# A masked sequence convolution in front of an fp8 feed-forward layer: x gathered in sorted order, transposed on TensorE, and convolved over the sequences that reach each chunk

## The chip, the cores and the metric

The kernel runs on one core of one Trainium2 chip. A time is the device time of one execution in microseconds (us); a kernel is given by the median of its runs. The engines are PE (TensorE: matmuls, with PEld for its weight loads), DVE (VectorE), ACT (ScalarE), POOL (GpSimd) and SP (SyncE, which here only issues DMAs). ACT and POOL issue DMAs too; all DMAs run on the same 16 DMA engines.

## The reference, cut to what matters

x has the shape [128 sequences b, 32 heads h, 512 positions l], float32, and each sequence b has a length between 78 and 453. Per head there is a response K of 512 values, made from a few small parameters; x is convolved with it causally, x times D is added, and positions at or beyond the sequence's length become zero. The result goes through a feed-forward layer along l (512 to 1376 to 512) whose inputs are rounded to fp8, and is added to x:

```
K = _get_kernel(log_dt, C, log_A_real, A_imag, Lq)            # [32 heads, 512]
y = irfft(rfft(u, 1024) * rfft(K, 1024))[..., :512] + u * D[:, None]
y = y * mask                                                  # l < length[b]
gate_out = fp8(y) @ gate_w.T ; up_out = fp8(y) @ up_w.T       # 512 -> 1376
hidden = silu(gate_out) * up_out
return x + fp8(hidden) @ down_w.T                             # 1376 -> 512
```

## The kernel before

The 32 heads are worked in 8 groups of 4 (`G`, `HG`); P is 128 and l is cut into 4 chunks of 128 (`LC`). The convolution is a block-Toeplitz product: output chunk c takes K's block of distance c-c' times input chunk c', for all c' up to c.

**Sorting.** The sequences are put in order of length, longest first: `rank` (L424 to L426), the permutation matrix `perm` (L427, bf16) and the row numbers `index` (L450, L452). Chunk c is then needed only for its first `CAPS[c]` sequences (128, 124, 84, 40; `NQ` = 376 columns in all instead of 512). A check at the end (`fits`, L442 to L444, and `verdict`) would send the whole computation to the second branch `wide` if the lengths did not fit; with these inputs it does not run.

**One group.** A group has three stages on PE:

1. Convolution of 4 heads (`conv`, L567, with `convolve`, L481). x comes transposed by the host (`xT`: [l, h, b]) in `load_x` (`xg`, one DMA of 1 MB per group), and the sum of chunks 0 and 1 comes as two accumulating DMAs on POOL's queue (`load_sums`, `xs`). x is the stationary operand, K's blocks `st` move (two DMAs per head, `toeplitz`, L470 and L471, that read a padded copy of K in DRAM, `kpads`). A product that two pairs of blocks share, `sp` (L485), is made once, copied by ACT (`shared`, L488), and added when DVE rounds the result to fp8 (`q`, L571). DVE then masks q by length (L581). The result is [b, l].
2. `sort` (L584): four fp8 matmuls per head with `perm` as the moving operand turn q into [l, sorted b] (`pq`), and ACT copies the 376 columns to `qs` (L596). `check_q` (L598) sums |q| on ACT to find numbers that are not finite.
3. `gate_up` (L625): 11 steps of 8 matmuls (L641, weights stationary, fp8 `qs` moving) into the PSUM tiles `gp` and `up`, two buffers each; ACT makes silu (`s`, L649), DVE the product (`v`, L651), and `quantise` (ACT L616, DVE L617 to L619) rounds it to `hq`. `Down.multiply` (L680) makes 11 matmuls of 512 columns per head from `hq`; `put_out` (L693) adds x (`xn`, gathered in the sorted order by `load_sorted`, an indirect DMA, L459) and scatters the rows to the output (L699, L697).

**Order.** The stages overlap by an order that is written out: the loop over g issues gate_up of group g, then, between the `down` matmuls of g, the convolution of g+1. `with after(x)` makes an instruction issue behind x on its engine. Work that isn't part of a group is strewn in: K of heads 4 to 15 (`others[0]`) in the prologue, K of heads 16 to 31 (`others[1]`) in groups 0 to 2, `low_halves` on ACT (L537).

**Queues.** SP issues the small inputs, `xg`, the weights and all of `st`. In group 0's gate_up, `first_loads` issues x of group 1 and both parts of `downT` from ACT (L116, L139, L144), and the sums and the first gather from POOL. In the prologue 22 matmuls that do nothing (`keep_busy`, L361) fill PE while K goes to DRAM and back.

**End.** The last group's output goes out in five scatters (three of 512 columns, two of 256, L697), each issued by POOL when its part is done.

Of the kernel before, what the change touches and what calls it, by code (L numbers as in the profile page):

```python
# [57 lines left out]
def ssm_fp8_ffn(  # L58
# [30 lines left out]
    CHUNKS = [3, 1, 2, 0]  # L89

# [8 lines left out]
    def chunk_of(g, c):  # L99
        return xT[c * P : (c + 1) * P, g * HG : (g + 1) * HG, :].rearrange("p h b -> p (h b)")  # L100


    def add_chunks(xg):
        xs = xp.tile([P, T], F32, name="xs", bufs=1)
        nc.vector.tensor_add(xs, xg[:, 0, :], xg[:, 1, :])
        return xs

    def load_sums(g):

        xs = xp.tile([P, T], F32, name="xs", bufs=1)  # L110
        nc.gpsimd.dma_start(xs, chunk_of(g, 1))  # L111
        return xs, nc.gpsimd.dma_start(xs, chunk_of(g, 0), accum_op=ALU.add)

    def load_x(g, queue=nc.sync):
        xg = xp.tile([P, LC, T], F32, name="xg", bufs=1)
        queue.dma_start(  # L116
            xg.rearrange("p c (h b) -> p c h b", b=B),
            xT[:, g * HG : (g + 1) * HG, :].rearrange("(c p) h b -> p c h b", p=P),
        )
        return xg  # L120

    sc = const.tile([P, 6], F32, name="sc")
    nc.sync.dma_start(sc, scales.to_broadcast([P, 6]))

    len_i = const.tile([P, B + 1], I32, name="len_i")
    nc.sync.dma_start(len_i[:, 0:B], lens.to_broadcast([P, B]))
    nc.sync.dma_start(len_i[:, B:], bass.AP(lens.tensor, lens.offset, [[1, P], [1, 1]]))
    x0 = load_x(0)
# [19 lines left out]
    load_gate_up(gw, gateT, 0, I2)  # L148

# [12 lines left out]

    RB, RZ = 2 * P // NB, P // NB
    NR = 2 * RB + NA
# [28 lines left out]
    gas = [kg.tile([P, w, NR + RZ], F32, name=f"ga{n}") for n, w in enumerate((HG, HB))]  # L193
# [44 lines left out]
    class Powers:  # L238
# [67 lines left out]
        def products(self):  # L306
# [6 lines left out]
            yield nc.vector.tensor_mul(sin, sin, self.be.unsqueeze(2).to_broadcast(S))  # L313

            ga = self.ga = gas[min(self.n, 1)][:, 0 : self.H, :]
            k0 = NR - NA
            yield nc.vector.tensor_add(ga[:, :, k0:NR], sin, cos)

            def pair(c0, step):
                a = ga[:, :, c0 : c0 + RB]  # L320
                return bass.AP(a.tensor, a.offset, [*a.ap[:-1], [step, 2], a.ap[-1]])


            yield nc.vector.tensor_sub(pair(0, RB), pair(k0, RB), pair(k0 + RZ, 0))

        def response(self, behind=None):
            kp = ps.tile([NR, self.H, NB], F32, name="kp", tag="dp")
            for j in range(self.H):
                nc.tensor.matmul(kp[:, j, :], self.ga[:, j, 0:NR], self.zb[:, j, :], start=j == 0, stop=False)
            done = nc.tensor.matmul(kp[:, :, NB - 1], last, sm[0:1, 5, self.hs], start=False, stop=True)  # L330
            kt = kts[self.n]
            with after(behind) if behind else ExitStack():
                copied = nc.vector.tensor_copy(kt[0:NR], kp)
            written = nc.sync.dma_start(kpads[self.n].rearrange("h (a b) -> a h b", b=NB), kt)
            return done, copied, written
# [25 lines left out]
    with after(done):  # L361
        keep_busy(22)
# [23 lines left out]
    l_i = kg.tile([P, L], I32, name="l_i")  # L386
    mask = const.tile([P, L], U8, name="mask")
# [3 lines left out]

    shared = [const.tile([P, 2, P], F32, name=f"shared{n}") for n in range(HG)]

    many = kg.tile([P, 1], F32, name="many")
    with after(first_done):
        nc.vector.memset(many, float(B))
    with after(coeffs_there):
# [4 lines left out]
        for t in shared:  # L402
            nc.gpsimd.memset(t[:, 1, :], 0.0)
        gpsimd_there = nc.gpsimd.tensor_scalar(key, lf, many, None, ALU.mult)
    with after(gpsimd_there):
        nc.gpsimd.tensor_add(key, key, col_f)
        for s, c in enumerate(CHUNKS):
            nc.gpsimd.iota(l_i[:, s * P : (s + 1) * P], pattern=[[-1, P]], base=(c + 1) * P - 1, channel_multiplier=0)
        mask_there = nc.gpsimd.tensor_scalar(mask, l_i, own, 255.0, ALU.is_lt, ALU.mult)
# [8 lines left out]
    perm = const.tile([P, B], BF16, name="perm")  # L418
    number = kg.tile([P, 1], BF16, name="number")
    counted = kg.tile([P, B], F32, name="counted")  # L420
    index = const.tile([P, 1], I32, name="index")
    with after(copied):
        xs0 = add_chunks(x0)
# [4 lines left out]
    with after(mask_there):  # L428
# [6 lines left out]
        nc.gpsimd.tensor_scalar(number, col_f[:, B:], -1.0, B - 1.0, ALU.mult, ALU.add)  # L435
        nc.gpsimd.iota(row_i, pattern=[[P, LC]], base=P - 1, channel_multiplier=-1)
        nc.gpsimd.tensor_copy(row_f, row_i)
# [8 lines left out]
    def indices(behind):  # L446

        op = ps.tile([P, 1], F32, name="op", tag="dp")
        with after(behind):
            nc.tensor.matmul(op, perm, number, start=True, stop=True)  # L450
        yield
        nc.vector.tensor_copy(index, op)  # L452

# [3 lines left out]
    def load_sorted(g):  # L457
        xn = xp.tile([P, HG * L], F32, name="xn", bufs=2)
# [6 lines left out]
    def toeplitz(pool, h):  # L465

        n = next(n for n, (_, h1) in enumerate(batches) if h < h1)
        st = pool.tile([P, 5, P], F32, name="st")
        kpad, at = kpads[n], kpads[n].offset + (h - batches[n][0]) * KP
        done = nc.sync.dma_start(st[:, 1:4, :], bass.AP(kpad.tensor, at + 5 * P, [[1, P], [1, 3 * P]]))  # L470
        done = nc.sync.dma_start(st[:, 0:5:4, :], bass.AP(kpad.tensor, at, [[1, P], [2 * P, 2], [1, P]]))  # L471
        return st, done

# [493 lines left out]
```

## Time and profile before

| | us |
|---|---|
| median of 3 runs (lowest to highest) | 312.45 (312.18 to 313.72) |
| the profiled execution | 312.24 |
| its span, first to last instruction | 310.5 |
| PE busy in the span | 286.3 |
| DVE busy | 264.7 |
| ACT busy | 183.7 |
| POOL busy | 47.2 |
| bytes moved by DMA | 48.48 MB |

In a row of the timeline the columns are the start, the duration, the engine, the line of the kernel, the operation, what it writes and reads, how many instructions were merged into the row, and in square brackets how long the engine had been idle and what released it. A matmul's recorded duration contains the way through the array, which overlaps with the next matmul; what a matmul costs in a stream is the distance from its start to the next one's start. A float32 matmul appears as two records (two passes), each with a weight load of its own.

### The profile page before, as it was taken

What the parts mean: (1) busy time and instruction counts of PE and PEld (TensorE: products, weight loads), DVE (VectorE), ACT (ScalarE), POOL (GpSimd) and SP (SyncE); (2) the same over time, 40 slices, a digit from 0 to 9 for tenths busy, and PEclk for the clock granted to TensorE, in tenths of its full rate; (3) what the DMA queues carried; (4) which work ended last, traced back from release to release, by engine and by line L of the source; (5) the groups of instructions that cost most, each with busy time, mean ns of one, the idle gap of its engine ahead of it and who ended that gap; (6) DMA issues with size and microseconds to landing.
All of it is one profiled execution on the core that took longest, in us unless ns stands there. A gap on an engine that the chain in (4) does not pass through costs nothing. (4 is left out here: it accounts for less than half of the span.)

```text
span 310.5 us, 4833 instructions
## 1 busy us (share of the span) xinstructions
PE 286.3 (92%) x1692; PEld 173.3 (56%) x1708; DVE 264.7 (85%) x465; ACT 183.7 (59%) x388; POOL 47.2 (15%) x96
## 2 busy tenths in 40 slices
PE   8999939995999999999999999999999999999870
PEld 3486517742577456745576457745674557555330
DVE  5895939795999999986999699969998799989980
ACT  5835725497855878288846486458816683578100
POOL 5740111021000210021003100030002110000042
PEclk9999987997999999999999999999999999999995
DMA  2599999594016930488036911593049640000033
GB/s 87 194 276 380 375 288 359 149 271 203 0 42 160 284 161 0 100 260 292 4 80 191 314 61 43 153 309 140 1 116 267 260 136 2 0 0 2 1 157 122
DMA packets 27987, 48.48 MB, mean 156 GB/s; under 512 B 3348, under 2 KB 17428, under 8 KB 26036
## 3 DMA queue, kind: packets, MB, share of 16 engines
q1 hardware_dynamic: 21940, 23.78, 26.9%
q0 software_dynamic: 4064, 20.45, 19.1%
q10 hardware_dynamic: 1952, 3.87, 3.4%
q8 instruction: 15, 0.25, 0.3%
q14 instruction: 16, 0.13, 0.1%
HBM read 39.55 MB, written 8.54 MB: 155 GB/s over the span
## 5 line engine op out<-in xcount | busy, mean ns | idle before, releaser
L680 PE MATMUL dp<-dw,hq 128*128 128x512 bf16 (+1 forms) x348 | 81.1, 380 | 3.9 <-DVE hq L619 2.4
L641 PE MATMUL gp<-qs,gw 128*128 128x512 fp8e4 (+1 forms) x352 | 71.7, 326 | 9.0 <-ACT s L649 8.4
L649 ACT ACTIVATE s<-gp,psc 128x512 f32<-128x512 f32 x88 | 58.7, 680 | 34.0 <-PE gp L641 27.8
L651 DVE SCALAR_TENSOR_TENSOR v<-up,psc,s 128x512 f32<-128x512 f32 x88 | 64.4, 748 | 16.0 <-ACT s L649 16.0
L641 PE MATMUL up<-qs,uw 128*128 128x512 fp8e4 (+1 forms) x352 | 71.9, 327 | 0.4
L680 PEld LDWEIGHTS <-hq 128*128 128x128 bf16 x363 | 33.1, 96 | 44.3 <-DVE hq L619 7.4
L618 DVE SCALAR_TENSOR_TENSOR hq<-m,v 128x1024 bf16<-128x1024 bf16 (+1 forms) x56 | 55.6, 993 | 1.1
L617 DVE SCALAR_TENSOR_TENSOR v<-m,v 128x1024 f32<-128x1024 bf16 (+1 forms) x56 | 55.4, 990 | 1.0 <-ACT m L616 1.0
L616 ACT ACTIVATE m<-v 128x1024 bf16<-128x1024 f32 (+1 forms) x56 | 48.7, 870 | 7.2 <-DVE v L651 7.1
L641 PEld LDWEIGHTS <-gw 128*128 128x128 bf16 x352 | 32.3, 98 | 35.8 <-issue 10.4
L641 PEld LDWEIGHTS <-uw 128*128 128x128 bf16 x352 | 32.5, 99 | 27.2 <-issue 2.6
L596 ACT ACTIVATE qs<-pq 128x376 fp8e4<-128x376 f32 x32 | 14.6, 479 | 28.0 <-PE pq L588 28.0
L693 DVE SCALAR_TENSOR_TENSOR xn<-dp,nsc,xn 128x512 f32<-128x512 f32 (+1 forms) x33 | 23.0, 730 | 8.8 <-PE dp L680 8.7
L488 ACT ACTIVATE shared<-sp,inv 128x128 f32<-128x128 f32 x32 | 11.5, 361 | 29.5 <-PE sp L485 29.5
L571 DVE SCALAR_TENSOR_TENSOR q<-cp,inv,shared 128x512 fp8e4<-128x512 f32 x32 | 23.8, 744 | 3.1 <-PE cp L494 2.9
L111 POOL DMA_DIRECT2D xs<-xT x7 | 4.4, 623 | 119.3 <-PE sp L485 119.2
L619 DVE TENSOR_SCALAR hq<-hq 128x1024 bf16<-128x1024 bf16 (+1 forms) x56 | 20.9, 373 | 1.4
L490 PE MATMUL cp<-st,xg 128*128 128x256 f32 x64 | 19.6, 388 | 0.0
L491 PE MATMUL cp<-st,xg 128*128 128x256 f32 x64 | 19.5, 387 | 0.0
L492 PE MATMUL cp<-st,xg 128*128 128x256 f32 x64 | 19.2, 382 | 0.0
L699 POOL DMA_INDIRECT out<-xn,index x7 | 7.6, 1084 | 75.3 <-DVE xn L693 70.9
L602 ACT ACTIVATE s<-q 128x1024 bf16<-128x1024 fp8e4 x16 | 16.7, 1054 | 0.0
(156 smaller groups left out, 286.5 us busy)
## 6 DMA issues: line engine op xcount, KB each, us to landing
xg<-xT SPq DMA_DIRECT2D x7, 1024.0 KB, 7.5
st<-kpad SPq DMA_DIRECT2D x32, 192.0 KB, 3.6
st<-kpad SPq DMA_DIRECT2D x32, 128.0 KB, 3.8
xs<-xT POOLq DMA_DIRECT2D x14, 256.0 KB, 5.1
dw<-downT ACTq DMA_DIRECT2D x2, 1280.0 KB, 8.0
gw<-gateT SPq DMA_DIRECT2D x2, 768.0 KB, 8.3
gw<-gateT SPq DMA_DIRECT2D x1, 1216.0 KB, 12.9
uw<-upT SPq DMA_DIRECT2D x1, 1216.0 KB
```

The source lines that it names most:

```text
L490: nc.tensor.matmul(cp[:, 1:4:2, :], xg[:, 0, b], st[:, 2:4, :], start=True, stop=False)
L491: nc.tensor.matmul(cp[:, 0:4:2, :], xg[:, 2, b], st[:, 2:4, :], start=False, stop=False)
L571: nc.vector.scalar_tensor_tensor(q[:, j, :].rearrange("p (k c l) -> p k c l", k=2, c=2), cp.rearrange("p (k c) l -> p k c l", k=2), inv[:, ...
L616: nc.scalar.activation(m, v, AF.Abs, scale=2.0**20 * (1.0 + 2.0**-6), accum_out=acc)
L617: yield nc.vector.scalar_tensor_tensor(v, m, 1.5 * 2.0**14, v, ALU.max, ALU.add)
L618: yield nc.vector.scalar_tensor_tensor(out, m, 1.5 * 2.0**14, v, ALU.max, ALU.subtract)
L619: yield nc.vector.tensor_scalar(out, out, FP8_MAX, -FP8_MAX, ALU.min, ALU.max)
L641: multiplied = nc.tensor.matmul(o[:, :, 0 : CAPS[c]], w[:, c, i * P : (i + 1) * P], qs[:, :, OFF[c] : OFF[c] + CAPS[c]], start=(c == 0), s ...
L649: gated = nc.scalar.activation(s, gp, AF.Silu, scale=pgate)
L651: done = nc.vector.scalar_tensor_tensor(v[:, (i - i0) * T : (i - i0 + 1) * T], up, pup, s, ALU.mult, ALU.mult)
L680: done = nc.tensor.matmul(self.dps[n], self.hq[:, i, j * B : (j + 1) * B], dm[:, i, l0:l1], start=(i == 0), stop=(i == IC - 1),)
L693: added = nc.vector.scalar_tensor_tensor(o, self.dps[n], ndown, o, ALU.mult, ALU.add)
```

## The change

- **x.** `xT` is read no more (outside `wide`). For each group the rows of x come once, in sorted order, by the indirect DMA that fetched them before for the final addition (`load_sorted`); for group 0 they come unsorted by a plain DMA first, and a second time sorted. Per head, four float32 transposes on TensorE (`by_length`: 128, 124, 84 and 40 rows of x stationary, an identity matrix moving) turn the needed sequences into [l, sorted b]; in group 0 four float32 matmuls with `perm` do it. ACT copies the 376 columns to SBUF (`take`).
- **Convolution.** K's blocks are now stationary and x moves: one float32 matmul of 376 columns for the diagonal, then six of 124, 84, 40, 84, 40 and 40 columns. The sum of chunks, the shared product, the subtraction in `products` and POOL's accumulating DMAs go away. The padded K is shorter, and `st` comes in one DMA of 256 KB per head, four in a row for a whole group (`load_k`).
- **Rounding.** ACT makes fp8 directly from PSUM into `qs` (`quantise_y`), and DVE masks 376 bytes per partition instead of 512. `sort` goes away; the mask is made in sorted order on DVE from a sorted copy of the lengths. `check_q` sums 752 columns instead of 1024 and runs for the group before.
- **Order.** Two heads' transposes stand at the start of the convolution stage, then 10 `down` matmuls, then the four convolutions with the other two heads' transposes between them.
- **Queues.** All weights, K and `downT` are loaded on SP's queue, in the order x of group 0, first parts of gate and up, K of group 0, the rest of gate and up, K of group 1, `downT`. ACT issues only the small inputs (at the very start). POOL issues the gathers, the write of the second K to DRAM and the scatters. The `xn` tile has three buffers, `qs` three.
- **Prologue and end.** `keep_busy(22)` becomes `keep_busy(7)`; the mask's work on POOL becomes work on DVE. The last group's output goes out in two scatters (1536 and 512 columns).

The core of the diff:

```diff
-    def load_sums(g):
-        xs = xp.tile([P, T], F32, name="xs", bufs=1)
-        nc.gpsimd.dma_start(xs, chunk_of(g, 1))
-        return xs, nc.gpsimd.dma_start(xs, chunk_of(g, 0), accum_op=ALU.add)
...
+    x0 = rows_of_x()
+    nc.sync.dma_start(x0, xb[0])
...
     load_gate_up(gw, gateT, 0, I2)
+    load_gate_up(uw, upT, 0, I1)
...
     with after(done):
-        keep_busy(22)
+        keep_busy(7)
...
+    sorted_lengths = ps.tile([P, B], F32, name="sl", tag="cp")
+    nc.tensor.matmul(sorted_lengths, lengths, perm, start=True, stop=True)
+    order = ps.tile([P, 1], F32, name="op", tag="dp")
+    nc.tensor.matmul(order, perm, number, start=True, stop=True)
...
+        st = pool.tile([P, LC, P], F32, name="st")
+        kpad = kpads[n]
+        return st, nc.sync.dma_start(st, bass.AP(kpad.tensor, kpad.offset + (h - batches[n][0]) * KP, [[1, P], [1, LC * P]]))
...
+            def by_length(g, j, xn):
+                xp_ = ps.tile([P, NQ], F32, name="xp", tag=("gp", "up")[j % 2])
                 for c in range(LC):
+                    o, n = xp_[:, OFF[c] : OFF[c] + CAPS[c]], CAPS[c]
+                    x = xn[:, j * L + c * P : j * L + (c + 1) * P]
+                    if g:
+                        done = nc.tensor.transpose(o, x[0:n], eye[0:n, 0:n])
+                    else:
+                        done = nc.tensor.matmul(o, x, perm[:, 0:n], start=True, stop=True)
+                return xp_, done
+
+            def take(xp_, before):
+                xt = xtp.tile([P, NQ], F32, name="xt")
+                with after(before) if before else ExitStack():
+                    return xt, nc.scalar.activation(xt, xp_, AF.Copy)
...
+            def conv(st, xt):
+                cp = ps.tile([P, NQ], F32, name="cp")
+                nc.tensor.matmul(cp, st[:, LC - 1, :], xt, start=True, stop=False)
+                for d in range(1, LC):
+                    for c in range(d, LC):
+                        done = nc.tensor.matmul(
+                            cp[:, OFF[c] : OFF[c] + CAPS[c]],
+                            st[:, LC - 1 - d, :],
+                            xt[:, OFF[c - d] : OFF[c - d] + CAPS[c]],
+                            start=False,
+                            stop=c == LC - 1 and d == LC - 1,
+                        )
+                return cp, done
+
+            def quantise_y(qs, j, cp, before, done):
+                with after(before) if before else ExitStack():
+                    made = nc.scalar.activation(qs[:, j, :], cp, AF.Copy, scale=inv[:, 0:1], saturate=False)
+                words = qs.bitcast(I32)[:, j, :]
+                with after(done) if done else ExitStack():
+                    return made, nc.vector.tensor_tensor(words, words, mask.bitcast(I32), ALU.bitwise_and)
...
             with after(loaded):
-                load_gate_up(uw, upT, 0, I1)
                 load_gate_up(gw, gateT, I2, IH)
                 load_gate_up(uw, upT, I1, IH)
                 load_gate_up(gw, gateT, IH, I)
-                load_gate_up(uw, upT, IH, I)
+                loaded = load_gate_up(uw, upT, IH, I)
+            with after(convolved):
+                others[0].response(done, nc.gpsimd)
+            with after(loaded):
+                sts, loaded = load_k(1)
+            with after(loaded):
+                load_down(0, EARLY)
+                load_down(EARLY, IC)
...
-            first_loads = {
-                2: lambda hq: loads.append(load_x(1, nc.scalar)),
-                3: sums_1,
-                5: lambda hq: loads.append(load_down(0, EARLY, nc.scalar)),
-                7: lambda hq: loads.append(load_down(EARLY, IC, nc.scalar)),
-                9: sorted_0,
-            }
+            first_loads = {3: rows(1, 0), 7: rows(0, firsts[1])}
...
+                for j in range(2):
+                    xp_, last = turn_head(j)
+                    xt, sent = take(xp_, sent)
+                    xts.append(xt)
+                for n in range(2):
+                    with after(last):
+                        last = d.multiply(n, 0, EARLY)
                 for j in range(HG):
+                    with after(last):
+                        cp, last = conv(sts[j], xts[j])
+                    if j < 2:
+                        xp_, last = turn_head(j + 2)
+                        xt, sent = take(xp_, sent)
+                        xts.append(xt)
                     if j in (0, 2):
                         with after(done):
                             *_, done = jobs.pop(0)
...
+                    sent, done = quantise_y(qs, j, cp, sent, done)
                 if g + 2 < G:
+                    sts, _ = load_k(g + 2)
+                    xns[g + 2] = load_sorted(g + 2)
...
+            check_q(G - 1, qs)
...
-    widths = [*(v.shape[1] for v in groups[:-1]), L, L, L, L // 2, L // 2]
+    widths = [*(v.shape[1] for v in groups[:-1]), 3 * L, L]
```

`rows(g, i)` issues the gather of group g's x from POOL once `hq[:, i]` of group 0 is there (a copy of one element on POOL waits for it); `turn_head(j)` calls `by_length` behind the last PE instruction.

## The prediction

> **What bounds the kernel now.** I read the page's busy times and slices first, to see which engine is full and where it is not:
>
> ```profile
> PE 286.3 (92%) x1692; PEld 173.3 (56%) x1708; DVE 264.7 (85%) x465; ACT 183.7 (59%) x388; POOL 47.2 (15%) x96
> ...
> PE   8999939995999999999999999999999999999870
> ...
> PEclk9999987997999999999999999999999999999995
> ```
>
> PE is full from slice 10 on. Its holes, and the slices with a low granted clock (PEclk), lie in the first quarter and at the end. So: the body is a sum of PE distances, the holes are waits. In the body gate_up starts at 174.34 us (group 4) and 271.61 (group 7), so a group takes 32.42 us; busy time by stretch gives PE 96.28 of these 97.27 us, an idle 0.3 us per group. Next the timeline, for what one head's convolution and sort cost PE there:
>
> ```profile
> 157.34 0.30 PEld L485 LDWEIGHTS sp<-st,xs 128*128 128x128 f32 x2
> ...
> 157.67 0.60 PE L490 MATMUL cp<-st,xg 128*128 128x256 f32 x2
> ...
> 158.10 0.59 PE L491 MATMUL cp<-st,xg 128*128 128x256 f32 x2
> ...
> 159.08 0.30 PEld L494 LDWEIGHTS cp<-st,xg 128*128 128x128 f32 x2
> ...
> 159.30 2.01 PEld L680 LDWEIGHTS <-hq 128*128 128x128 bf16 x10
> ...
> 163.52 0.32 PEld L588 LDWEIGHTS <-q 128*128 128x128 fp8e4 x4
> ...
> 163.77 0.30 PEld L485 LDWEIGHTS sp<-st,xs 128*128 128x128 f32 x2
> ```
>
> One convolution is 159.30 - 157.34 = 1.96 us, one sort 163.77 - 163.52 = 0.25: 2.21 us per head. A 256-column float32 matmul costs 158.10 - 157.67 = 0.43, or 0.84 ns per column and pass; a 128-column one 0.22 (159.08 to 159.30), 0.107 per pass. Then the first hole, on the same view, and the clock behind it in busy time by stretch:
>
> ```profile
> 39.56 0.80 PE L641 MATMUL up<-qs,uw 128*128 128x512 fp8e4 x4
> ...
> 43.76 0.38 ACTq L139 DMA_DIRECT2D dw<-downT  x1
> ...
> 44.81 1.27 ACT L649 ACTIVATE s<-gp,psc 128x512 f32<-128x512 f32 x2 [5.88 <-issue]
> ...
> 45.55 1.41 PE L641 MATMUL gp<-qs,gw 128*128 128x512 fp8e4 x4 [5.19 <-ACT s L649]
> ```
> ```profile
> 44.00:48.00 4.00, 2.45 (x8) 1.10 (x8) 2.47 (x4) 3.19 (x6) 0.00 (x0) 0.50 1.08 339
> 48.00:52.00 4.00, 4.00 (x19) 3.50 (x18) 3.35 (x6) 2.56 (x9) 1.09 (x1) 0.68 1.06 345
> ```
>
> ACT stood still until its DMA of downT was issued at 43.76 (DMA share about 1 there), so `s` was late, PE idled 5.19 us, and the granted clock (third number from the right) fell to 0.50. From 27.33 to 68.02, gate_up to gate_up, group 0 takes 40.69 us, 8.27 over the body's 32.42. Last, the end:
>
> ```profile
> 301.07 0.48 DVE L693 SCALAR_TENSOR_TENSOR xn<-dp,nsc,xn 128x256 f32<-128x256 f32 x1
> ...
> 304.54 0.97 POOL L697 DMA_INDIRECT out<-xn,index  x1 [0.30 <-issue]
> ```
>
> The last result is there at 301.55; POOL, at 1.28 us per scatter, issues the last one at 304.54.
>
> **The change, part by part.** Sums are made against the profiled run, 312.24 us (span 310.5 and 1.74 around it), 0.21 below the median of 312.45.
>
> *Convolution on PE.* 376 columns: 376 x 0.84 ns x 2 passes = 0.63 us. Six small ones (124 to 40 columns): no row has a float32 matmul with a full 128-column weight load and fewer than 128 moving columns. By columns alone they cost (124+84+40+84+40+40) x 1.68 ns = 0.69 us; if the weight load is the floor, each pass costs what a 128-column pass costs, 6 x 0.215 = 1.29. I take the floor: the float32 weight load is recorded at 190 to 195 ns for 128 columns and 112 ns for 32 columns (K's matmul, L329), so about 0.84 ns per column, 107 ns for 128. `keep_busy` has 52 weight loads for 51 matmuls with one weight, so a repeated weight is loaded again. Per head 1.92 (ends 1.32 and 1.92).
>
> *Transposes instead of sort.* Four per head, float32, not in the trace. Nearest rows: the fp8 sort, 0.062 each, and the two-pass float32 matmul, 0.215. I take one pass with a float32 weight load, 0.107, so 0.43 per head. Rows of the trace name the part of the array that is used (128*128, 128*32, 1*32); a 40-row transpose may use less than 128 rows. Where that part changes from 128*128 to 128*32 and to 1*32 (25.13 to 25.27, 26.02 to 26.15), PE lost 0.07 to 0.10. Two changes per head: 0.17. Together 0.60 (ends 0.25 and 0.86 + 0.17 = 1.03).
>
> The Trainium skill's page "TensorE: Matmul & The Clock Gate", section "Part 4: PE-mode transpose", speaks against this step: about 275 ns per bf16 transpose in a kernel, and the clock gate doesn't count it as work. By 275 ns the four would take 1.1 per head and not 0.43, and the sum below would be 19 us longer. No run so far shows a transpose; the 40-column fp8 matmul is recorded at 183 ns and costs 62, so I read 275 as a duration, not a distance.
>
> So a head takes 1.92 + 0.60 = 2.52 instead of 2.21, and a stage 4 x 0.31 = 1.24 more. DVE loses L571 (744 ns) and the mask shrinks from 292 ns (128 words) to an estimated 250 (94 words; 64 and 128 elements take DVE 225 and 279 ns): 0.79 per head, 3.1 per group, on an engine that is behind PE; the 0.3 us per group that PE idles should go (wait list: `hq` before L680). The two ACT copies per head (about 0.48 each by L596, for 0.36 + 0.48) lie beside PE: `xt` of heads 0 and 1 has 2.1 us of `down` matmuls as cover, that of 2 and 3 a convolution of 1.92; uncovered, each would cost 0.48. Net +0.94 per stage, 7 stages: **+6.6**.
>
> *Group 0.* ACT issues no DMA there, and xg, xs and a second x layout no longer move. From 17 us on the DMAs run at about 378 GB/s. K 1.05 MB and the rest of the weights 4.33 MB are in by about 31; the last of them is needed at 34. The 5.19 us wait and the slow clock go. What is late next: K of group 1, the gather of group 1 (issued at about 32 behind `hq[:,0]`, median 7.9 us to landing, so about 40) and half of downT, 3.4 MB, 9 us, against the first transpose at about 40. I reserve 0.8 (ends 0 and 5). The other wait of these groups, 3.25 us at 73.98, stays: ACT's sines wait for angles on DVE, which follow the put_outs. Gain 8.27 - 0.8: **-7.5**.
>
> The page "Trainium Kernel Development and Optimization", section "Key Constraints", says that queues share the 16 DMA engines and that several issuers save only issue time. Then the move to SP gives no bandwidth, and only the bytes count; the row above shows that the issue itself held ACT.
>
> *Prologue.* PE ends K's matmuls at 11.6; 7 fillers 1.5, order and 16 perm matmuls of 0.215 to about 17.0 (x0 and perm are there by 13.4), four convolutions 7.7, copy, mask and K's next batch about 1.4: gate_up at about 26.3 instead of 27.33, **-1.0**. 0.5 MB more ahead of K's round trip in SP's queue can take it back (ends 0 and -1.8). The four ACT copies are ahead of the sines; these wait for DVE anyway.
>
> *POOL and SP.* POOL loses 14 sum DMAs and the l mask; the gathers are issued a group ahead. SP's K loads come four in a row behind the weights; nothing else waits on SP. check_q of the last group lands on ACT, idle from 289: nothing; uncovered 2 us.
>
> *End.* Two scatters instead of five. The last would be issued at about 301.7, not 304.54, but the 2.1 MB of both groups move at up to 451 GB/s from 299.9 on and need until about 305, against 307.1 now: **-2.3** (ends 0 and -2.9).
>
> Sum: 312.24 + 6.6 - 7.5 - 1.0 - 2.3 = 308.0.
>
> **The rivals.**
> - *Transposes at the two-pass price* (ends slower). Place: the head of each convolution stage. 0.215 each plus the tile changes is 1.03 per head: +0.43 x 28 = +12.0, 320.0 us. It decides early: 4.2 us over 112 transposes, so above 0.145 each nothing is left, above 0.16 it is slower by 0.5%. For it: no single-pass float32 row exists. Against: only that a transpose does no arithmetic; no row.
> - *The clock drops in the stages.* By columns alone a head has 1.32 us of convolution and some 0.16 of transposes in 2.52 us, about 60% of PE's time. For it: after 3.25 us of idling the clock stood at 0.50 for some 3.4 us (74.7 to 78). Against: 56% busy (292.4 to 295.8) left it at 1.00. If each stage lost 1.7 us: +12, 320.
> - *The group-0 stall moves instead of going.* gather and downT arrive 5 us later than the first transpose: 308.0 + 4.2 = 312.2, no change. For it: POOL's 256 KB sum took 5 us at 33.4 under full DMA load.
> - *No weight-load floor.* 1.32 + 0.25 per head: 4 x (1.57 - 2.21) - 0.3 = -2.9 per stage, -20: 281. Against: the load durations above.
>
> **How the numbers follow.** 0.5% (1.56 us) is about what a measurement of this kernel tells from no change. Main case 0.50, of which nine tenths are under 310.9; transposes 0.16; clock 0.10; stall 0.12, half of it within 0.5%; no floor 0.07; 0.05 for a mishap that I don't see, slower. Faster 0.45 + 0.07 + 0.04 = 0.56, same 0.05 + 0.06 = 0.11, slower 0.33. Range: the good ends together (transposes 0.062 and no tile change, -9.8; reserve 0, prologue -1.8, end -2.9) give 312.24 - 3.2 - 8.3 - 1.8 - 2.9 = 296; I take 299, since not all fall together, and above the two slower rivals, 322. The main case alone: 304 to 311.
>
> **What would show it.** Right: no ACT wait for a DMA issue near 40 us and clock 1.00 there; gate_up of group 1 at about 60 instead of 68; a body of about 33.4 us per group; a small float32 matmul 0.215 from the next, a transpose 0.107; the last scatter issued near 302. Wrong: transposes 0.2 apart or more, PEclk below 9 in the stages, PE idle before the first transpose, `cp` or `xt` waits of PE on ACT.

## The result, and the profile after

The changed kernel takes 327.42 us (median of 4 runs, 326.61 to 328.22); the kernel before, in the same comparison, 312.89 (312.18 to 313.72). The ratio is 1.046, with a 95% interval of 1.042 to 1.050: slower, where 308.0 was forecast. The profiled execution has a span of 324.5 us, 14.0 more than before. Medians below are over all runs of a kernel, ratios leave out single runs more than 1.5% above the fastest of the same kernel (one each in e1, e4 and e6).

The page of the changed kernel, busy times and slices:

```profile
PE 296.8 (91%) x1776; PEld 176.0 (54%) x1776; DVE 240.4 (74%) x433; ACT 187.4 (58%) x388; POOL 31.2 (10%) x72
...
PE   6899934998899999999999999999999999999970
...
PEclk9999985999999999999999999999999999999996
```

DVE lost 24 us of work and PE gained 10.5. Between the first slice and the end PE has one large hole, in slices 6 and 7, and the granted clock falls only there. So the loss has two places: that hole, and something in the body that doesn't look like a hole.

The starts of gate_up, read from the timeline, cut both spans at the same points:

| | before | after | difference | forecast |
|---|---|---|---|---|
| up to the first gate_up | 27.33 | 28.05 | +0.7 | -1.0 |
| group 0 | 40.69 | 45.89 | +5.2 | -6.6 (-7.5 and one stage) |
| group 1 | 38.11 | 37.80 | -0.3 | +0.9 |
| groups 2 to 6 | 165.48 | 175.30 | +9.8 | +4.7 |
| last gate_up to the end | 38.89 | 37.45 | -1.4 | -2.3 |
| span | 310.5 | 324.5 | +14.0 | -4.2 |

Groups 3 to 5 are alike: 33.27 us before, 35.33 after. (The 32.42 per group of the prediction was a mean over groups 4 to 6, and group 6 lasts only 30.73, because its last `down` product moves behind the next gate_up. The body before was 0.85 longer than the prediction thought, and group 0's excess was 7.4 and not 8.27.)

Group 0 first. The timeline of SP's and PE's queues after:

```profile
34.34 3.72 SPq L437 DMA_DIRECT2D st<-kpad  x4
38.11 1.24 SPq L119 DMA_DIRECT2D dw<-downT  x2
39.39 4.48 SPq L124 DMA_DIRECT2D dw<-downT  x1
```
```profile
42.42 1.26 PE L502 MATMUL xp<-eye,xn 128*128 128x128 f32 x8
52.96 3.57 PE L631 MATMUL dp<-dw,hq 128*128 128x512 bf16 x8 [9.27 <-DMA dw<-downT]
```

The issue of downT from ACT is gone, and ACT waits for no issue there any more. In its place PE waits 9.27 us for downT itself, which SP issued only at 38.11, behind K's four blocks. The clock answers as it did before; by stretch (busy time of PE, PEld, DVE, ACT and POOL, granted clock, DMA share, GB/s):

```profile
44.00:48.00 4.00, 0.00 (x0) 0.00 (x0) 3.40 (x5) 1.46 (x5) 0.00 (x0) 0.77 1.02 404
48.00:52.00 4.00, 0.00 (x0) 0.00 (x0) 0.00 (x0) 0.00 (x0) 0.00 (x0) 0.50 1.01 406
52.00:56.00 4.00, 3.04 (x8) 1.06 (x8) 0.00 (x0) 0.00 (x0) 0.00 (x0) 0.50 0.87 289
```

Then the body; PE's timeline through one convolution stage (group 4), from the transposes of two heads to the next gate_up:

```profile
197.91 1.26 PE L502 MATMUL xp<-eye,xn 128*128 128x128 f32 x8
199.11 0.85 PE L631 MATMUL dp<-dw,hq 128*128 128x512 bf16 x3
200.16 1.75 PE L631 MATMUL dp<-dw,hq 128*128 128x512 bf16 x7 [0.21 <-DVE hq L567]
201.75 0.79 PE L526 MATMUL cp<-xt,st 128*128 128x376 f32 x2
202.38 1.43 PE L529 MATMUL cp<-xt,st 128*128 128x124 f32 x12
203.64 0.67 PE L502 MATMUL xp<-eye,xn 128*128 128x128 f32 x4
204.24 0.90 PE L526 MATMUL cp<-xt,st 128*128 128x376 f32 x2
204.98 1.43 PE L529 MATMUL cp<-xt,st 128*128 128x124 f32 x12
...
208.83 0.88 PE L526 MATMUL cp<-xt,st 128*128 128x376 f32 x2
209.55 1.43 PE L529 MATMUL cp<-xt,st 128*128 128x124 f32 x12
210.80 4.25 PE L631 MATMUL dp<-dw,hq 128*128 128x512 bf16 x18
215.24 3.79 PE L631 MATMUL dp<-dw,hq 128*128 128x512 bf16 x16 [0.20 <-DVE hq L567]
218.87 0.80 PE L589 MATMUL gp<-qs,gw 128*128 128x512 fp8e4 x4
```

By distances, four transposes cost 204.24 - 203.64 = 0.60. The 376-column product costs 202.38 - 201.75 = 0.63 where it follows `down`, 204.98 - 204.24 = 0.74 where it follows transposes, and 209.55 - 208.83 = 0.72 where it follows another convolution. The twelve small passes cost 203.64 - 202.38 = 1.26, 0.105 each, whether they have 124 columns, 84 or 40. Transposes and convolutions together are 10.25 us of this stage, 1.41 more than the 8.84 before (4 x 2.21). The 44 `down` matmuls have 10.71 against 10.06: the lists of waits, first of the changed kernel and then of the kernel before, have

```profile
PEld L631 <- DVE hq L567: 12.9, 21, 2.0
...
PE dp L631 <- DVE hq L567: 4.5, 14, 1.5
```
```profile
PEld L680 <- DVE hq L619: 7.4, 9, 2.0
```

(total, how often, the longest). 1.41 + 0.65 = 2.06, the whole difference of the body.

### The profile page after: what moved, and what is told of

Read it like the earlier page. It is cut to its first block, busy times and chain, and to the rows that moved or that the text cites. A ratio compares the mean times of both kernels' runs of the same rounds, so it can differ in the third digit from the quotient of the medians.

```text
span 324.5 us, 4852 instructions
## 1 busy us (share of the span) xinstructions
PE 296.8 (91%) x1776; PEld 176.0 (54%) x1776; DVE 240.4 (74%) x433; ACT 187.4 (58%) x388; POOL 31.2 (10%) x72
## 4 chain that ended last, share of the span: by engine, by line
PE 48%; DVE 29%; issue 8%; ACT 7%; DMA 6%; POOLq 0%; POOL 0%; SPq 0%; ACTq 0%; DVEq 0%
PE cp L529 12%; PE dp L631 12%; DVE v L599 9%; PE cp L526 7%; DVE v L565 6%; PE gp L589 6%; DVE hq L566 5%; PE up L589 5%; DMA dw<-downT 5%; ACT s L597 4%; DVE hq L567 3%; PE xp L502 3%; ACT m L564 2%; ACT qs L541 1%; DMA sm<-ssm 1%
## 5 line engine op out<-in xcount | busy, mean ns | idle before, releaser
L631 PE MATMUL dp<-dw,hq 128*128 128x512 bf16 (+1 forms) x363 | 86.2, 386 | 13.8 <-DMA dw<-downT 9.3
L631 PEld LDWEIGHTS <-hq 128*128 128x128 bf16 x363 | 33.8, 99 | 60.0 <-DVE hq L567 12.9
L529 PEld LDWEIGHTS cp<-xt,st 128*128 128x128 f32 x384 | 47.9, 192 | 8.1
L529 PE MATMUL cp<-xt,st 128*128 128x40 f32 (+2 forms) x384 | 45.7, 272 | 0.0
L544 DVE TENSOR_TENSOR qs<-qs,mask 128x94 int32<-128x94 int32 x32 | 8.2, 255 | 50.4 <-ACT qs L541 50.4
L510 ACT ACTIVATE xt<-xp 128x376 f32<-128x376 f32 x32 | 14.7, 481 | 47.7 <-PE xp L502 46.3
L649 POOL DMA_INDIRECT out<-xn,index x9 | 9.3, 1033 | 237.8 <-DVE xn L644 237.0
L541 ACT ACTIVATE qs<-cp,inv 128x376 fp8e4<-128x376 f32 x32 | 18.3, 571 | 22.1 <-PE cp L529 22.0
L526 PE MATMUL cp<-xt,st 128*128 128x376 f32 x64 | 27.8, 516 | 0.0
L502 PE MATMUL xp<-eye,xn 128*128 128x128 f32 (+1 forms) x112 | 18.3, 266 | 0.0
L502 PEld LDWEIGHTS xp<-eye,xn 128*128 128x128 f32 (+1 forms) x112 | 13.8, 150 | 4.3
```

Source lines behind the costliest of these rows:

```text
L502: done = nc.tensor.transpose(o, x[0:n], eye[0:n, 0:n])
L526: nc.tensor.matmul(cp, st[:, LC - 1, :], xt, start=True, stop=False)
L529: done = nc.tensor.matmul(cp[:, OFF[c] : OFF[c] + CAPS[c]], st[:, LC - 1 - d, :], xt[:, OFF[c - d] : OFF[c - d] + CAPS[c]], start=False, s ...
L631: done = nc.tensor.matmul(self.dps[n], self.hq[:, i, j * B : (j + 1) * B], dm[:, i, l0:l1], start=(i == 0), stop=(i == IC - 1),)
```

## The experiments

### downT ahead of K of group 1 (e1), and one gather later (e2)

The first theory for group 0: downT is late because it stands in SP's queue behind K's blocks, which wait for K's write. The rival: the bytes are too many, whatever their order.

```diff
             with after(loaded):
+                load_down(0, EARLY)
+                loaded = load_down(EARLY, IC)
+            with after(loaded):
                 sts, loaded = load_k(1)
-            with after(loaded):
-                load_down(0, EARLY)
-                load_down(EARLY, IC)
```

> Edit: in the changed kernel, SP issues the loads of downT right behind the gate and up weights, and K of group 1 after them. Nothing else. The changed kernel is at 327.4 us; there SP stood waiting for K's write to DRAM until 34.3 us, the DMAs were 0.20 busy from 32 to 36, downT was issued at 38.1 and was awaited by PE until 53.0 (9.3 us idle, then the clock at 0.50 until about 56). Theory H (downT is late because SP's queue was blocked in front of it): downT lands near 40, the 9.3 us wait and some 2 us of slow clock go, gate_up of group 1 starts near 63 instead of 73.9: 316 to 317 us. Rival R (the 16 DMAs have too much to move before 44 us: K 1, gathers 3, downT 2.8 MB): the wait only moves to K of group 1 or to the gather: 322 to 327 us.

319.95 us against 313.1 of the kernel before on that chip, ratio 1.018 (1.013 to 1.023); 7.5 less than the changed kernel. Group 0 fell from 45.89 to 38.22. The wait for downT is gone, as theory H said; its 316 to 317 us were not reached: the first gate_up came 1.1 later (29.13), and a shorter wait was left. What is late next is what the prediction had thought of, the gather of group 1. PE's timeline:

```profile
45.30 1.74 PE L502 MATMUL xp<-eye,xn 128*128 128x128 f32 x8 [1.63 <-DMA xn<-x,index]
```

The second run adds that the third gather (of group 2's x, which nothing needs for 30 us) waits on POOL for `hq[:, 7]`:

```diff
-                    xns[g + 2] = load_sorted(g + 2)
+                    with after(nc.gpsimd.tensor_copy(turn[:, 2:3], hq[:, firsts[4], 0:1])) if g == 0 else ExitStack():
+                        xns[g + 2] = load_sorted(g + 2)
```

> Edit: as the run before (downT ahead of K of group 1), and the gather of group 2's x, which POOL issued at 41 us right behind that of group 0, now waits for hq[:,7] of group 0. Theory H: the same 316 to 317 us, since what mattered was when downT was issued. Rival R (bytes): the third megabyte out of the way gives another 2.5 us where the run before still has a wait for a DMA in group 0, and nothing where it has none.

319.45 us, ratio 1.020 (1.016 to 1.024); group 0 37.72. The two runs can't be told apart. The order in the queue was the fault, not that gather.

### The 40-row transposes made 128 rows (e3)

PE's records name the part of the array that an instruction uses: 128*128, 124*128 and 84*128 for the first three transposes of a head, 40*128 for the last. The prediction had charged two changes of shape per head. Here the 40-row transposes get 128 rows; the extra columns aren't read:

```diff
-                xp_ = ps.tile([P, NQ], F32, name="xp", tag=("gp", "up")[j % 2])
+                xp_ = ps.tile([P, L], F32, name="xp", tag=("gp", "up")[j % 2])
...
-                        done = nc.tensor.transpose(o, x[0:n], eye[0:n, 0:n])
+                        if n < 64:
+                            n = P
+                        done = nc.tensor.transpose(xp_[:, OFF[c] : OFF[c] + n], x[0:n], eye[0:n, 0:n])
```

> Edit: the transpose of the fourth chunk takes all 128 rows of x (into spare columns of the PSUM bank) and not 40, so that all four have the same tile 128*128. In the changed kernel the distances in one head are 0.11 and 0.12 between transposes of 128, 124 and 84 rows, 0.16 to 0.17 into the 40-row one and 0.18 out of it. Theory T (the change of tile costs): 0.11 everywhere, 0.13 less per head, 28 heads: 323.8 us, 0.45 per head. Rival (a price of the short transpose or of the switch between transposes and matmuls): 327 us, no change.

323.31 us, ratio 1.032 (1.028 to 1.036). More work, less time. The same place of PE's timeline, one head's transposes and the product behind them:

```profile
203.93 0.60 PE L504 MATMUL xp<-eye,xn 128*128 128x128 f32 x4
204.37 0.80 PE L528 MATMUL cp<-xt,st 128*128 128x376 f32 x2
205.00 1.43 PE L531 MATMUL cp<-xt,st 128*128 128x124 f32 x12
```

The transposes cost 0.44 instead of 0.60, and the product behind them 0.63 instead of 0.73. The fourth head's product, which follows a convolution, stays at 0.71. The body fell by 0.53 only, from 35.33 to 34.80: PE now reaches the `down` matmuls earlier, and waits longer for `hq` (16.0 us instead of 12.9).

The Trainium skill's page "TensorEngine Tiling (Array Packing)", section "Key Properties", says that a change of the tiling mode drains TensorE. The trace fits that: transposes of 128, 124 and 84 rows are 0.11 to 0.14 apart, and 0.17 and 0.18 lie before and behind the start of the 40-row one. But this run takes away the short transpose together with the change of shape, so it gives their price and doesn't show that a drain is the cause. The product behind them costs as much behind another convolution (0.72), where all records have 128*128.

### DVE's jobs ahead of the masks (e4)

DVE works in the order that is written out. In the changed kernel each mask (L544) stands between two of DVE's rounding jobs, and waits for a convolution that comes later than before, because `down` matmuls and transposes are ahead of it. DVE's timeline in the stage shown above:

```profile
202.53 0.43 DVE L567 TENSOR_SCALAR hq<-hq 128x1024 bf16<-128x1024 bf16 x1
205.33 0.26 DVE L544 TENSOR_TENSOR qs<-qs,mask 128x94 int32<-128x94 int32 x1 [2.38 <-ACT qs L541]
207.92 0.26 DVE L544 TENSOR_TENSOR qs<-qs,mask 128x94 int32<-128x94 int32 x1 [2.34 <-ACT qs L541]
208.10 1.22 DVE L565 SCALAR_TENSOR_TENSOR v<-m,v 128x1024 f32<-128x1024 bf16 x1
```

DVE idles 4.72 us ahead of a job (208.10), and `hq` is late for `down`. In PE's timeline of that stage the lateness shows twice: three `down` matmuls at 199.11 take 1.05 us, 0.37 more than at 0.227 each, and the 18 at 210.80 take 4.44, 0.35 more. The edit has two parts, one for each place. It takes both jobs before the first mask, and it puts `down` over 3 blocks of `hq` instead of 5 ahead of the convolutions:

```diff
-                        last = d.multiply(n, 0, EARLY)
+                        last = d.multiply(n, 0, firsts[2])
...
-                    if j in (0, 2):
-                        with after(done):
-                            *_, done = jobs.pop(0)
+                    if j == 0:
+                        for _ in range(2):
+                            with after(done):
+                                *_, done = jobs.pop(0)
...
-                        last = d.multiply(n, EARLY, LATE)
+                        last = d.multiply(n, firsts[2], LATE)
```

> Edit: in the convolution stage both quantise jobs are issued at head 0, ahead of DVE's masks, where the second stood behind the mask of head 1; and the first down matmuls of the stage go over 3 of the 11 blocks of hq instead of 5. In the changed kernel DVE stood still 2.4 and 2.3 us per stage in front of masks, and PE's down matmuls in a stage took 10.7 us for 44 at 0.227, 0.7 more than their distances. Theory D (hq is late because DVE's order puts masks that wait for PE in front of it): 0.7 less in 7 stages, 322.5 us, body 34.6 per group. Rival (DVE's order costs nothing; the 0.7 are fixed prices of switching): 327 us, body 35.3.

322.51 us, ratio 1.028 (1.026 to 1.031); the body 34.61, 0.73 less than 35.34. The second job starts at 202.40 in the same stage of this run, with no mask in front of it:

```profile
202.40 1.22 DVE L565 SCALAR_TENSOR_TENSOR v<-m,v 128x1024 f32<-128x1024 bf16 x1
```

The list of waits of this run:

```profile
PEld L631 <- DVE hq L567: 3.1, 2, 2.0
...
PE dp L631 <- DVE hq L567: 2.1, 2, 1.5
```

What is left of it is two waits, at the end of the kernel. So the waits in the body came from order: about half from the order on DVE, an engine that has less to do than before, and about half from `down` matmuls placed ahead of the rounding of their blocks. The halves are read from the timeline; no run has one part of the edit without the other.

### The small loads on SP again (e5, e11)

The changed kernel issues `len_i` and `sc` from ACT at the very start, beside `sm` on SP. All of K's arithmetic waits for `sm`.

```diff
-    nc.scalar.dma_start(len_i[:, 0:B], lens.to_broadcast([P, B]))
+    nc.sync.dma_start(len_i[:, 0:B], lens.to_broadcast([P, B]))
...
-    nc.scalar.dma_start(sc, scales.to_broadcast([P, 6]))
+    nc.sync.dma_start(sc, scales.to_broadcast([P, 6]))
```

> The changed kernel with the loads of len_i and sc on SP's queue again, behind sm, as before the change; 327.4 us without this edit. Theory S: the small loads that ACT issues beside sm make sm land at 4.69 us instead of 2.75, and all of the prologue is that much later; then sm lands at about 2.75 here, the first gate_up starts at about 26.1 instead of 28.05, and the time is about 325.5. Rival: sm is late for another reason (x0 is issued behind it in the same queue); then sm still lands at about 4.7, the first gate_up starts at about 28, and the time is 327.4.

DVE's first instruction, in the changed kernel and then in this run:

```profile
4.69 0.20 DVE L35 TENSOR_SCALAR ex_k<-sm 128x64 int32<-128x64 f32 x1 [4.69 <-DMA sm<-ssm]
```
```profile
2.74 0.20 DVE L35 TENSOR_SCALAR ex_k<-sm 128x64 int32<-128x64 f32 x1 [2.74 <-DMA sm<-ssm]
```

The first gate_up starts at 26.25 instead of 28.05. The time is 326.19, ratio 1.043 (1.037 to 1.049); the 1.2 us to the changed kernel, where 1.9 were expected, can't be told from nothing by these intervals. In the profiled execution group 0 took 0.8 of the earlier start back: PE waits 10.0 us for downT, 9.27 in the changed kernel.

Two things had changed at once here, since x of group 0 (1 MB) now came out 1.4 us later too. The other order, with the small loads behind x, tells them apart:

```diff
     nc.sync.dma_start(x0, xb[0])
+    nc.sync.dma_start(len_i[:, 0:B], lens.to_broadcast([P, B]))
...
+    nc.sync.dma_start(sc, scales.to_broadcast([P, 6]))
```

> The changed kernel with the loads of len_i and sc on SP's queue, behind x of group 0 instead of ahead of it. In the run with the small loads right behind sm, two things had changed at once: ACT issued nothing beside sm, and the 1 MB of x came out 1.4 us later. Theory S (ACT's small loads hold sm up): sm lands at about 2.75 and the first gate_up starts at about 26.3. Rival (x, issued 0.46 us behind sm, holds it up): sm lands at about 4.7 and the first gate_up starts at about 28.

`sm` is there at 2.83 and the first gate_up starts at 26.11 (326.57 us in one execution): theory S. It was the loads that ACT issued, not x. The other traces say the same: `sm` is there between 4.69 and 5.92 in the five kernels in which ACT issues the small loads (the changed one, e1 to e4) and between 2.71 and 2.83 in the eight in which SP does.

### Parts of the change alone, in the kernel before (e7, e8, e9)

The end: two scatters of 1536 and 512 columns instead of five.

```diff
+                    self.sent = [(g, n, 0, HG * L)] if g < G - 1 else [(g, HG - 2, 0, last), (G, n, last, HG * L)]
...
-    widths = [*(v.shape[1] for v in groups[:-1]), L, L, L, L // 2, L // 2]
+    widths = [*(v.shape[1] for v in groups[:-1]), 3 * L, L]
```

> One part of the change alone, in the kernel before: the last group's output in two scatters (1536 and 512 columns) instead of five. The forecast's term: -2.3 us, 310.6 from 312.9. Rival, from the stretch from the last gate_up to the end, 38.89 us before and 37.45 after the change: -1.4, 311.5. A second rival: the bytes of the last two groups set the end; then less than 0.5 us of difference.

312.93 us against 312.69, ratio 0.999 (0.995 to 1.002): the number of the second rival, but not its reason, since the bytes are out earlier (from 306 to 308 us 14 GB/s move here, 92 in the kernel before). POOL does issue the last scatter earlier, at 301.58 instead of 304.54, but it lands 5.8 us after its issue, where the last two of before take 3.7 in the median, and the span ends 3.8 us after that landing instead of 2.3. What those last microseconds are made of, the trace doesn't tell.

Group 0: downT on SP behind the weights, and no DMA issued by ACT behind x of group 1.

```diff
                 load_gate_up(uw, upT, IH, I)
+                load_down(0, EARLY)
+                load_down(EARLY, IC)
...
-                5: lambda hq: loads.append(load_down(0, EARLY, nc.scalar)),
-                7: lambda hq: loads.append(load_down(EARLY, IC, nc.scalar)),
```

> One part of the change alone, in the kernel before: both loads of downT issued by SP behind the weights instead of by ACT in group 0's gate_up; x of group 1 stays on ACT. Theory A (the forecast's term): ACT's wait of 5.9 us on the issue goes, PE's wait of 5.2 and the slow clock go with it, and at most 0.8 us of a new wait comes: 305.4 from 312.9, group 0 about 33.2 instead of 40.7. Theory B: with downT ahead, x of group 1, its sums and K of group 1 (about 3 MB) come 2 to 4 us late for the first convolution; group 0 is then 36 to 38 and the time 308 to 310. Theory C: ACT's next DMA issue (x of group 1) blocks in the same way behind downT's bytes; then the waits only move and the time stays at 312.9.

316.34 us, ratio 1.011 (1.005 to 1.016), and none of the three theories: 1% slower than the kernel before. The timeline of SP and of PE:

```profile
21.86 8.16 SPq L139 DMA_DIRECT2D dw<-downT  x2
30.07 5.84 SPq L144 DMA_DIRECT2D dw<-downT  x1
36.00 1.63 SPq L334 DMA_DIRECT2D kpad<-kt  x1
49.02 0.35 SPq L470 DMA_DIRECT2D st<-kpad  x1
```
```profile
52.16 0.77 PE L485 MATMUL sp<-st,xs 128*128 128x128 f32 x2 [9.81 <-DMA st<-kpad]
```

ACT's wait is gone, as theory A said. But SP is held up until 35.9 issuing downT, as ACT had been, with the DMA share above 1; now K's write (27.06 before) stands behind it, with everything that reads K behind that. The last part on its own moves this write to POOL:

```diff
-                *_, written = others[0].response(made)
+                *_, written = others[0].response(made, nc.gpsimd)
```

> The kernel before with downT on SP behind the weights (316.3 us, PE waiting 9.8 us for K's blocks of group 1) and, beside that, the write of K of heads 4 to 15 to DRAM issued by POOL instead of SP. Theory Q: the 9.8 us came from the order in SP's queue, K's write standing behind downT's issues until 36.0; POOL writes K at about 31, the blocks are issued from about 37, and group 0 falls from 45.6 us to 36 to 38: 308 to 310 us. Theory Y: the bytes ahead of the first convolution set the wait (weights, downT, x of group 1, sums and K all have to come through engines that are full until about 46); then group 0 stays at 41 or more and the time at 313 or more.

314.94 us against 313.72 in that comparison, ratio 1.004 (1.001 to 1.007). K is written at 27.64 and its blocks are issued from 35.27, yet PE waits 7.35 us for one of them, at 42.1 to 49.4, with the DMA share above 1 from 28 to 48. Group 0 takes 42.76: both signs of theory Y, that the DMAs don't get x of group 1, its sums, K and downT in by the first convolution. That holds for the two orders tried. K's blocks still stood behind downT on SP here (it was issued until 35.16), and K's blocks ahead of downT were not tried.

### All edits together (e6, e10)

The edits are downT before K, the later gather, the padded transposes, DVE's jobs ahead, and the small loads on SP.

> All edits together: downT loaded ahead of K of group 1 and the third gather held back until hq[:, 7] (-8.0 us alone), the 40-row transposes padded to 128 rows (-4.1), DVE's jobs ahead of the masks with only the heads' first part of down before the convolutions (-4.9), and the small loads on SP (-1.9 expected). If the causes are separate, the sum is 327.4 - 8.0 - 4.1 - 4.9 - 1.9 = 308.5 us, the body 34.1 per group, group 0 about 38, the first gate_up at about 26.1. Rival: they share their cover (PE's waits for hq come back as the transposes get shorter, and an earlier start makes the gather of group 1 later against its use); then the body is 34.5 or more and the time is 312 or more.

307.85 us (median of 5 runs), ratio 0.982 (0.976 to 0.988) to the kernel before: the sum had said 308.5. The body came out better than the sum, 33.68. In e3 the padding alone had lost part of its gain to PE's waits for `hq`. Here it keeps all of it: from the first transpose to the end of the last convolution a stage takes 209.04 - 197.43 = 11.61 us in e4 and 199.05 - 188.37 = 10.68 here, 0.93 less; with the 0.73 of e4 that is the 1.66 by which the body fell.

The profiled execution of this kernel took 312.68 us, the other four 306.16 to 307.99. Its trace has a hole again: PE waits 2.25 us for one of K's blocks, the granted clock is 0.50 in 48 to 56, and group 0 takes 42.70.

```profile
46.70 0.97 PE L528 MATMUL cp<-xt,st 128*128 128x376 f32 x2 [2.25 <-DMA st<-kpad]
```
```profile
48.00:52.00 4.00, 4.00 (x18) 3.42 (x18) 0.49 (x2) 0.95 (x2) 1.14 (x2) 0.50 0.18 31
```

The other four executions have no trace; as they are 4.7 to 6.5 us shorter, their hole must be smaller or missing. The last run puts K's blocks between the two parts of downT, since the second part is wanted only behind the convolutions:

```diff
             with after(loaded):
-                load_down(0, EARLY)
-                loaded = load_down(EARLY, IC)
+                loaded = load_down(0, EARLY)
             with after(loaded):
                 sts, loaded = load_k(1)
+            with after(loaded):
+                load_down(EARLY, IC)
```

> The run with all edits, with K of group 1 between the two parts of downT instead of behind both: the second part is wanted only after the convolutions. In the profile of the run with all edits PE waits 1.4 us for the gather of group 1 and 2.2 us for K's blocks, the second wait is followed by a granted clock of 0.50 from 48 to 56 us, and the other runs of that kernel were at 306.2 to 308.0. Theory O: order is what is left; the wait for K's blocks goes, the clock stays at 0.9 or more in 48 to 56, group 0 is about 37, and the time is 305 to 307. Theory Y (bytes): the gather and the second part of downT come as much later as K's blocks come earlier; PE waits 2 us or more elsewhere in group 0 and the time stays at about 307.9.

304.05 us (303.76 to 304.61 in 6 runs), ratio 0.970 (0.967 to 0.973): faster than both kernels. Theory O, and better than it said, though against the usual execution of e6 the new order is worth about 4 us and not the 8.5 by which group 0 differs between the two traces. The slices of the page, and busy time by stretch where the hole was:

```profile
PE   8999999989999999999999999999999999999880
...
PEclk9999999999999999999999999999999999999996
```
```profile
44.00:48.00 4.00, 4.00 (x35) 3.71 (x34) 3.90 (x5) 0.98 (x3) 0.00 (x0) 1.00 1.03 342
48.00:52.00 4.00, 4.00 (x30) 3.37 (x29) 1.02 (x4) 1.65 (x4) 1.14 (x2) 1.00 0.67 169
```

Group 0 takes 34.18 us, 0.5 more than a group of the body, and PE waits 0.31 in it for the gather and for no other DMA. No slice has a low clock before the end. Against the kernel before the span is 8.9 shorter: 1.3 up to the first gate_up, 6.5 in group 0, 2.0 in group 1, 1.2 at the end; the body is still 0.4 per group longer.

## Why the prediction was wrong, point by point

- **Group 0, -7.5: the step that failed.** The prediction had the mechanism right as far as ACT went (no wait for a DMA issue, as it said) and named what is late next, "K of group 1, the gather of group 1 (...) and half of downT", but priced the three together by their bytes, with a reserve of 0.8; "only the bytes count" was the step. It said of SP: "SP's K loads come four in a row behind the weights; nothing else waits on SP." downT waited on SP, behind those K loads, and these behind K's way through DRAM. That wait was 9.27 us, with the clock at 0.50 from 48 to 56, and group 0 grew by 5.2. Put in another order (e1) it fell by 7.7. With the order of the last run it is 34.18, 0.5 over a group of the body, where the kernel before has 7.4. So the size forecast was there to be had, but by the order in one queue, which the prediction hadn't traced. In the kernel before, the two orders tried didn't bring it (e8, e9); that the bytes are too many there is likely and not shown.
- **Rival "the group-0 stall moves instead of going", 312.** This is what happened, and the prediction gave it 0.12. Its place was wrong (the first transpose, instead of the first `down` behind it), and its price, 5 us, was too low.
- **The stages, +0.94 each: right in its parts, too small in the sum.** Convolution 1.89 to 2.00 per head, 1.92 forecast. The floor that was taken from the weight load is there: 0.105 per pass for 40 to 124 columns, so the rival without it is out. Four transposes cost 0.60, as forecast (0.43 and 0.17; 0.44 and 0.16 by e3). Not counted: the 376-column product costs 0.72 to 0.74 in three heads of four, 0.63 in the first. In all 1.41 per stage, 1.24 forecast. The rest is the relief of 0.3 that was to come from a lighter DVE, and came as a loss of 0.65: the prediction counted DVE's instructions, but not what stands in front of what, on DVE and on PE (e4). Over the groups 2 to 6 the difference was 9.8 instead of 4.7.
- **The base of 32.42.** It was averaged over groups that aren't alike. It didn't enter the sum except through group 0's excess, 8.27 instead of 7.4.
- **Prologue, -1.0: right but for one load.** Forecast 26.3; 28.05 came, and 26.25 and 26.11 with the small loads on SP (e5, e11). The list of the change says that ACT issues "only the small inputs"; the prediction never asked whom they delay.
- **End, -2.3.** 1.4 came in the changed kernel, and nothing measurable in the kernel before (e7). There the scatter is issued 2.96 earlier and the bytes are out earlier, as the prediction had it, but the span doesn't end with the bytes: it ends 9.6 us after the last issue, 6.0 in the kernel before. Why stays open.
- **The rivals on price.** Without the short one, transposes are 0.11 apart on average (0.44 for four in e3), not 0.215. The clock is 1.00 in the stages (174.34 to 207.60: 32.78 of 33.26 us busy, clock 1.00). A transpose's record lasts 236 to 306 ns here, while a quarter of 0.44 is what it costs in a stream. The Trainium skill's page "TensorE: Matmul & The Clock Gate", section "Part 4: PE-mode transpose", has about 275 ns for one in bf16; that is near the length of a record here, and not near a cost. That the clock gate doesn't count them can't be told from these runs, where transposes stand in lots of four or eight between matmuls.

## What to carry to other kernels

When transfers move into one queue, write down that queue in order, with the time at which each entry can start and the time at which it is wanted; an entry that waits for something (here K's way through DRAM) holds back all behind it. A long wait of PE costs twice: at 5.19 us (before) and 9.27 (after) the clock went to 0.50. When an in-order engine gets less work, read what each of its instructions now waits for before counting the relief: the mask was cheaper and stood in the way of a job. A body's period is to be read from two equal groups, not from a mean that takes in the last one.

## What had not been expected of the hardware

- Three small loads, issued at 0.73 to 1.66 us by ACT, made a 96 KB load that SP issued at 0.73 be there only at 4.69 (5.92 in e1); behind it in SP's queue they leave it at 2.74 (e5) or 2.83 (e11).
- A transpose of 40 rows is dearer than one of 128: 0.16 to 0.20 per head in the transposes, and 0.10 in the product where it comes directly behind them (two heads of four). In all 0.93 us for a stage (e4 against the run with all edits).
- A DMA issue can hold up the engine that issues it while the DMAs are busy (DMA share about 1): ACT for 5.9 us in the kernel before, SP until 35.9 in e8. Moving the issue moves what it holds.
- A wait of under 2 us can be followed by a slow clock, or not. PE waits 1.63 us for the gather in e1 and 1.80 in e2, at the same place and followed by the same matmuls. In e1 the clock stands at 0.50 from 46 to 49 us, in e2 it stays at 1.00 (a stretch of e1, the same of e2, and PE's wait in e2):

```profile
44.00:48.00 4.00, 2.70 (x11) 1.60 (x12) 3.96 (x5) 1.99 (x6) 0.00 (x0) 0.71 1.05 371
```
```profile
44.00:48.00 4.00, 2.55 (x14) 1.48 (x15) 3.96 (x5) 2.26 (x6) 0.00 (x0) 1.00 1.05 379
```
```profile
45.45 1.29 PE L502 MATMUL xp<-eye,xn 128*128 128x128 f32 x8 [1.80 <-DMA xn<-x,index]
```

In the profiled execution of e6 1.43 and 2.25 us of waiting were followed by 0.50, in e10 0.31 by 1.00. So the length of a wait alone doesn't settle it, and what does isn't shown.
